# A graph attention layer on one core: x_r of 32 nodes as f32 rows beside the edge attributes, in one product over 64 rows

## The chip, the cores and the metric

The kernel runs on one core of a Trainium2 chip. The metric is device microseconds of one execution, on that core; the time before is the median of three runs. A core has five engines that run side by side and wait for each other by semaphores: PE (TensorE, matrix products out of SBUF into the PSUM banks; PEld in the profile is its loading of weights), DVE (VectorE), ACT (ScalarE), POOL (GpSimd, here nearly only the issuer of gathers from DRAM) and SP (which here issues all other transfers).

## The reference, cut to what matters

One pre-norm GATv2 layer with a feed-forward block over 12500 nodes of 128 features, 8 heads of 16 channels, and 400000 edges sorted by destination, with 32 attributes each:

```
h   = relu(layernorm(x));  g = LN1(h)
x_l = g @ W_l ;  x_r = g @ W_r ;  e = edge_attr @ W_e          # 128 wide
m     = leaky_relu(x_l[src] + x_r[dst] + e, 0.2)
alpha = sum over channels of m * att                            # 8 per edge
a     = softmax of alpha over the edges (and one self loop) of each dst
h2    = h + sum over edges of a * x_l[src] + bias
out   = x + h2 + gelu(LN2(h2) @ W1 + b1) @ W2 + b2
```

Self loops take the mean edge attribute. Everything is f32.

## The kernel before, in words

**Stages.** A first part (lines 701 to 761) normalises the nodes, computes x_l and writes it to DRAM (`xl_dram`, rows of 136 floats); meanwhile POOL gathers raw rows of x for 29 later groups of edges (L277, 116 gathers), from which x_l of those edges is recomputed later, so that the main loop need not gather them. x_r of later nodes is computed inside the main loop, four node tiles at a time (`xr_steps`, eight steps, one per round): it is split into three bf16 parts whose sum is the f32 value (`first`, `second`, `third`, L586 to L597), and stored to `xs_dram`, three rows of 128 bf16 per node.

**Main loop** (`window_edges`). The edges are cut into tiles of 128, two tiles make a unit (at most 16 destination nodes), two units a pair of 512 edges (at most 32 destination nodes, the window). There are 782 pairs. A round r runs every stage once, each for its own pair: the table `stages` (L1312) and `late_stages` say how many rounds a stage lies behind, and the order in the table is the order in which each engine gets its instructions; nothing is reordered. The node finish (`steps`, `soon`, `last_steps`) and the x_r and raw steps are put behind the stages in fixed rounds.

For pair c:
- `gather` (four rounds ahead, L907): four indirect transfers, 128 rows of `xl_dram` each, into the tile `xs`. Twelve `xs` tiles go round. The 29 pairs with recomputed rows load them from `late_dram` by SP instead, so 3009 gathers remain.
- `windows` (three rounds ahead, L923), on SP: once in four pairs the edge attributes `ea` (32 attributes of pair q on partitions 32q to 32q+31, 128 partitions in all) and `dlw`: on 96 partitions the distance of each edge's destination from the pair's first one, on 16 more from its unit's first one. Every pair: `xrw`, the 96 bf16 rows of its 32 nodes.
- `place` (one round ahead, L940): one DVE compare makes `ne`, 112 rows of 512 bf16 ones and zeros. Rows 3n to 3n+2 say that the edge goes to node n of the window; the 16 rows behind say that it goes to node n of its unit.
- `combine` (L954): in one PSUM bank `z`, four transposes of the gathered x_l, plus `xrw` times `ne` in bf16 (which picks x_r), plus `we_z` times `ea` in f32 (`we_z[q]` is W_e on the 32 rows of pair q and zero on the other 96).
- `slope` and `bend`: leaky relu, ACT and DVE, one round later, into `m`.
- `score` (two rounds behind, L976): in the bank `ab`, `farw` times `ne` (a huge number for the nodes of the unit that the edge does not go to) minus `m` times att. `lowest` (DVE) and `weigh` (ACT): minimum and exponentials `p` per node and head. `turn`, `keep_turned`, `collect`: transposes of `p`, and the weighted sums of `xs` into the bank `acc`. `own_heads` and `put` pick the own heads and store the sums.

Four rings of two PSUM banks each serve all this: `z`, `ab`, `pt_ps`, `acc`. The order of PE in a round is combine, turn, collect, score. DVE's is own_heads, lowest, bend, place, and then the steps of the node finish, among them `f_biases` (L1110, L1112) and `f_rest` (L1211), each an addition of two SBUF operands, and `f_out`, which takes a bank of the ring `ab` for two rounds. `f_z` reads x_r of its nodes from `xs_dram` and adds the three parts by 12 bf16 products with the identity for four tiles.

## Time and profile before

| what | value |
|---|---|
| three runs | 4013.26, 4021.4 (median), 4024.89 us |
| the profiled execution | 4009.67 us, of which the span 4007.9 |
| mean granted TensorE clock | 0.956 |
| busy: PE, DVE, ACT, POOL | 3550.4, 2540.8, 2185.3, 2993.8 us |
| moved by transfers | 566.02 MB, 141 GB/s on average |
| first and last gather of the main loop start at | 161.6 and 3950.8 us |

The profile is one execution. A row of a group gives line, engine, operation, output and inputs by the program's names, how often, then the busy time in us and the mean of one in ns, and behind the bar the idle time of that engine just before, with what ended it; `issue` there means that the engine waited for nothing that the profile shows. A row by line gives the shortest, median and longest of one in ns, and when the first and the last started. A row of the timeline gives start and length in us. The chain is followed back from the last instruction, at each step to what released it.

### The profile page before, as it was taken

To read this page: it belongs to the slowest core of one execution; us is meant where nothing else is said; L and a number is where in the kernel's file an instruction comes from. 1 tells how busy PE (TensorE), PEld (TensorE's weight loads), DVE (VectorE), ACT (ScalarE), POOL (GpSimd) and SP (SyncE) were. 2 spreads that over 40 slices of the span, in tenths; PEclk is the share of its full clock that TensorE was granted. 3 is DMA by queue.
4 is the path that set the end of the run, shared out by engine and by line. 5 is a ranking of instruction groups with operands and counts; after the bars stand their busy time and mean duration, and the time that the engine had idled before them with its cause. 6 is when DMAs were issued, how large, how long until landed. Compare 5 with 4: busy or idle time off the path is not lost.

```text
span 4007.9 us, 63213 instructions
## 1 busy us (share of the span) xinstructions
PE 3550.4 (89%) x19116; PEld 2520.3 (63%) x19315; DVE 2540.8 (63%) x5940; ACT 2185.3 (55%) x4768; POOL 2993.8 (75%) x3153
## 2 busy tenths in 40 slices
PE   3488998998889999998998999999989989998997
PEld 3356666666666666666666666666666666666665
DVE  7467676767666665665666666566666656566565
ACT  7445555555555545555555555556555455554554
POOL 7777777777777777777777777777777777777773
PEclk7699999999999999999999999999999999999998
DMA  7677787677656655555556556555556555655553
GB/s 215 207 186 193 197 206 201 173 178 170 166 122 132 128 125 127 126 124 125 118 126 133 125 124 128 128 125 120 127 118 130 125 115 123 127 118 124 125 116 72
DMA packets 650171, 566.02 MB, mean 141 GB/s; under 512 B 385806, under 2 KB 524925, under 8 KB 649581
## 3 DMA queue, kind: packets, MB, share of 16 engines
q1 hardware_dynamic: 549245, 344.42, 34.1%
q0 software_dynamic: 100000, 217.32, 27.4%
q8 instruction: 156, 2.56, 0.3%
q14 instruction: 194, 1.59, 0.1%
q10 hardware_dynamic: 576, 0.13, 0.0%
HBM read 492.44 MB, written 69.02 MB: 140 GB/s over the span
## 4 chain that ended last, share of the span: by engine, by line
PE 43%; DMA 21%; POOL 20%; issue 11%; DVE 1%; ACT 0%; SPq 0%; POOLq 0%; DVEq 0%; ACTq 0%
DMA xs<-xl_dram,src_sb 21%; POOL xs L915 20%; PE z L963 10%; PE acc L1021 9%; PE ab L981 8%; PE pt_ps L1007 5%; PE z L959 5%; PE z L962 2%; PE ab L980 1%; PE acc L1295 1%; PE acc L1270 1%; PE acc L1131 0%; PE pt_ps L581 0%; PE pt_ps L668 0%; PE acc L1126 0%
## 5 line engine op out<-in xcount | busy, mean ns | idle before, releaser
L915 POOL DMA_INDIRECT xs<-xl_dram,src_sb x3009 | 2873.2, 955 | 917.2 <-issue 792.8
L999 ACT ACTIVATE p<-ab,rec 128x256 f32<-128x256 f32 x1563 | 655.2, 471 | 1057.4 <-DVE rec L988 1041.1
L1030 DVE TENSOR_TENSOR own<-acc,diag 128x272 f32<-128x272 f32 x782 | 344.1, 440 | 1077.3 <-PE acc L1021 1061.6
L1021 PE MATMUL acc<-xs,pt 128*128 128x136 f32 x6250 | 881.0, 286 | 2.4 <-DVE f_o L1190 2.2
L959 PE MATMUL z<-ident,xs 128*128 128x128 f32 x3125 | 561.9, 283 | 342.6 <-DMA xs<-xl_dram,src_sb 338.6
L959 PEld LDWEIGHTS z<-ident,xs 128*128 128x128 f32 x3125 | 398.4, 142 | 741.1 <-DMA xs<-xl_dram,src_sb 410.8
L963 PE MATMUL z<-ea,we_z 128*128 128x512 f32 x1564 | 839.7, 620 | 0.1
L981 PE MATMUL ab<-m,negrep 128*128 128x512 f32 x1564 | 802.3, 595 | 11.4 <-issue 1.3
L1021 PEld LDWEIGHTS acc<-xs,pt 128*128 128x128 f32 x6250 | 809.3, 197 | 3.8 <-issue 3.5
L1012 ACT COPY pt<-pt_ps 128x512 f32<-128x512 f32 x782 | 455.1, 582 | 591.0 <-PE pt_ps L1007 581.6
L1007 PEld LDWEIGHTS pt_ps<-ident,p 128*128 128x128 f32 x3125 | 410.9, 147 | 439.3 <-issue 394.4
L988 DVE TENSOR_REDUCE rec<-ab 128x2 f32<-128x512 f32 x781 | 540.4, 692 | 124.0 <-PE ab L981 116.6
L974 DVE TENSOR_TENSOR m<-z,zs 128x512 f32<-128x512 f32 x782 | 532.8, 681 | 87.2 <-ACT zs L969 85.7
L969 ACT ACTIVATE zs<-z 128x512 f32<-128x512 f32 x782 | 472.6, 604 | 44.1 <-DMA xs<-xl_dram,src_sb 35.7
L1007 PE MATMUL pt_ps<-ident,p 128*128 128x128 f32 x3125 | 492.7, 283 | 1.2 <-ACT p L999 1.2
L1036 DVE TENSOR_REDUCE rec<-own 128x34 f32<-128x272 f32 x782 | 340.9, 436 | 26.7
L963 PEld LDWEIGHTS z<-ea,we_z 128*128 128x128 f32 x1564 | 308.1, 197 | 32.7
L981 PEld LDWEIGHTS ab<-m,negrep 128*128 128x128 f32 x1564 | 301.6, 193 | 40.2 <-issue 4.3
L962 PE MATMUL z<-ne,xrw 128*128 128x512 bf16 (+1 forms) x781 | 304.8, 390 | 0.2 <-DMA xs<-xl_dram,src_sb 0.2
L945 DVE TENSOR_SCALAR ne<-dlw,nid 112x512 bf16<-112x512 bf16 x782 | 288.2, 369 | 13.5 <-DMA dlw<-du_dram 13.5
L980 PE MATMUL ab<-ne,farw 128*128 128x512 bf16 x585 | 223.8, 383 | 2.5 <-ACT p L999 1.6
L277 POOL DMA_INDIRECT raw<-in_x,src_raw x116 | 116.6, 1005 | 38.0 <-issue 34.1
(246 smaller groups left out, 2317.4 us busy)
## 6 DMA issues: line engine op xcount, KB each, us to landing
dlw<-dc_dram SPq DMA_DIRECT2D x196, 384.0 KB
ea<-in_ea_t SPq DMA_DIRECT2D x196, 256.0 KB
ea_s<-in_ea_t SPq DMA_DIRECT2D x98, 512.0 KB
xs<-xl_dram,src_sb POOLq DMA_INDIRECT x3009
state<-rec SPq DMA_DIRECT2D x1563, 9.0 KB
xrw<-xs_dram SPq DMA_DIRECT2D x782, 24.0 KB
state<-empty SPq DMA_DIRECT2D x28, 504.0 KB
f_st<-state SPq DMA_DIRECT2D x48, 288.0 KB
```

Of the source, the lines that this page charges most:

```text
L915: nc.gpsimd.indirect_dma_start(out=xs[:, j, :], out_offset=None, in_=xl_dram, in_offset=bass.IndirectOffsetOnAxis(ap=src_sb[:, c * KP + j ...
L959: nc.tensor.matmul(z[:, j * P : (j + 1) * P], d["xs"][:, j, 0:P], ident, start=(j == 0), stop=False, is_transpose=True)
L962: nc.tensor.matmul(z[:, :e], xrw[c % NV], d["ne"][:, :e], start=False, stop=False)
L963: nc.tensor.matmul(z[:, :e], we_z[:, c % QP, :], d["ea"][:, :e], start=False, stop=True)
L969: nc.scalar.activation(d["zs"][:, :e], d["z"][:, :e], AF.Copy, scale=SLOPE)
L974: nc.vector.tensor_tensor(d["m"][:, :e], d["z"][:, :e], d["zs"][:, :e], op=OP.max)
L981: nc.tensor.matmul(ab[:, :e], negrep.rearrange("p n h -> p (n h)"), d["m"][:, :e], start=False, stop=True)
L988: nc.vector.tensor_reduce(d["rec"][:, :, CX], d["ab"].rearrange("p (u e) -> p u e", e=U), AX.X, OP.min)
L999: nc.scalar.activation(d["p"][:, us], d["ab"][:, us], AF.Exp, bias=d["rec"][:, i, CX:SH], scale=-1.0)
L1007: nc.tensor.transpose(d["pt_ps"][:, js], d["p"][:, js], ident)
L1012: nc.scalar.copy(d["pt"][:, :e], d["pt_ps"][:, :e])
L1021: nc.tensor.matmul(d["acc"][:, i, :], d["pt"][:, j * P : (j + 1) * P], d["xs"][:, j, :], start=(j == js[0]), stop=(j == js[-1]),)
```

## The change

- x_r is no longer split. `xr_steps` has six steps: `keep` copies the product to SBUF in f32 and `store` writes it to `xr_dram`, one row of 128 floats per node. The window of a pair is 32 rows of 512 bytes.
- A pair now uses one half of the 128 partitions, even pairs rows 0 to 63, odd pairs rows 64 to 127. In its half, 32 rows hold the edge attributes and 32 rows the ones and zeros for the nodes, now f32 and written by `place` into the tile `ea` itself. The matching weights `zw` hold W_e on 32 rows and the 32 x_r rows behind; `combine` makes one f32 product over these 64 rows in place of the bf16 product and the f32 product over 128 rows.
- The 16 rows for the nodes of the unit lie in the other half (for even pairs rows 64 to 79, for odd ones rows 0 to 15). `place` makes them for two pairs at once, in `ne`, by a bf16 compare over 96 partitions, once in two pairs. The product of `farw` with them is a stage of its own, `apart`, right behind `combine` and over the other 64 rows; it opens the bank `ab`, and `score` adds the f32 product.
- `windows` issues, once in four pairs, two transfers for `ea` and four for `dl` (32 rows of window distances and 16 of unit distances per half) in place of one and two; each pair's window goes to its half of `zw`.
- `f_z` adds x_r by four f32 products with the identity in place of 12 in bf16.
- The memsets of `xrw` on POOL go; DVE prepares `zw`, `ne` and `dl`. The constants for the third parts, `ident_b` and `we_z` go, others for the halves come.

```diff
-NS = 3
+HALF = P // 2
-XR_STEPS = 8
+XR_STEPS = 6
...
-        def first(d):
+        def keep(d):
             n = d["n"]
-            xr = d["b"][:, 0 : n * P].rearrange("p (t f) -> p t f", f=P)
-            d["parts"] = pool.tile([P, GN, NS, P], BF16, name="xr_parts")[:, 0:n]
-            nc.scalar.copy(d["parts"][:, :, 0, :], xr)
-            nc.vector.tensor_sub(tile_of(d, "left", 0), xr, d["parts"][:, :, 0, :])
-
-        def second(d):
-            nc.scalar.copy(d["parts"][:, :, 1, :], d["left"][:, 0 : d["n"]])
-
-        def third(d):
-            nc.vector.tensor_sub(d["parts"][:, :, 2, :], d["left"][:, 0 : d["n"]], d["parts"][:, :, 1, :])
+            d["xr"] = pool.tile([P, GN, XW], F32, name="xr_rows")[:, 0:n, 0:P]
+            nc.scalar.copy(d["xr"], d["b"][:, 0 : n * P].rearrange("p (t f) -> p t f", f=P))
...
-        for t in xrw:
-            nc.gpsimd.memset(t, 0.0)
+        for t in zws:
+            nc.vector.tensor_copy(t, weh)
         for t in nes:
-            nc.vector.memset(t, 1.0)
+            nc.vector.memset(t, 0.0)
+        for t in dls:
+            nc.vector.memset(t, float(NW))
...
+                ea = load.tile([P, QP // 2, EPR], F32, name="ea")
+                dl = dls[c // QP % ND]
+                for i in range(2):
+                    h, at = i * HALF, (c + i) * EPR
+                    nc.sync.dma_start(
+                        ea[h : h + DE], bass.AP(
+                            tensor=ea_t.tensor, offset=ea_t.offset + at, ap=[[e_pad, DE], [2 * EPR, QP // 2], [1, EPR]]
+                        ),
+                    )
+                    for rs, of in ((slice(h + DE, h + DE + CW), dc_dram), (slice(HALF - h, HALF - h + NW), du_dram)):
+                        nc.sync.dma_start(
+                            dl[rs], bass.AP(
+                                tensor=of.tensor, offset=of.offset + at,
+                                ap=[[0, rs.stop - rs.start], [2 * EPR, QP // 2], [1, EPR]],
+                            ),
+                        )
...
         def place(c):
 
             d = pairs[c]
-            n, q = sum(edges_of(c)), c % QP * EPR
-            ne = nes[c % NN]
-            nc.vector.tensor_scalar(
-                ne[0 : NC3 + NW, :n],
-                d["dlw"][:, q : q + n],
-                nid[0 : NC3 + NW],
-                None,
-                op0=OP.is_equal,
-            )
-            d["ne"] = ne
+            rs = slice(d["half"].start + DE, d["half"].stop)
+            nc.vector.tensor_scalar(d["ea"][rs], d["dl"][rs], nid[rs], None, op0=OP.is_equal)
+            if c % 2 == 0:
+                nc.vector.tensor_scalar(d["ne"][0 : P - DE], d["dl"][0 : P - DE], nid[0 : P - DE], None, op0=OP.is_equal)
...
-            nc.tensor.matmul(z[:, :e], xrw[c % NV], d["ne"][:, :e], start=False, stop=False)
-            nc.tensor.matmul(z[:, :e], we_z[:, c % QP, :], d["ea"][:, :e], start=False, stop=True)
+            rs = d["half"]
+            nc.tensor.matmul(z[:, :e], d["zw"][rs], d["ea"][rs, :e], start=False, stop=True)
             d["z"] = z
+
+        def apart(c):
+            d, e = pairs[c], sum(edges_of(c))
+            d["ab"] = ps2.tile([P, EPR], F32, name="ab")
+            rs = d["other"]
+            nc.tensor.matmul(
+                d["ab"][:, :e], farw.rearrange("p n h -> p (n h)")[rs], d["ne"][rs, :e], start=True, stop=False
+            )
...
-            ab = ps2.tile([P, EPR], F32, name="ab")
-            nc.tensor.matmul(ab[:, :e], farw.rearrange("p n h -> p (n h)"), d["ne"][:, :e], start=True, stop=False)
-            nc.tensor.matmul(ab[:, :e], negrep.rearrange("p n h -> p (n h)"), d["m"][:, :e], start=False, stop=True)
-            d["ab"] = ab
+            nc.tensor.matmul(d["ab"][:, :e], negrep.rearrange("p n h -> p (n h)"), d["m"][:, :e], start=False, stop=True)
...
             (0, combine),
+            (2, apart),
             (4, turn),
```

126 lines of the change are left out of this document (55 added, 71 removed).

## The prediction

> **What bounds the kernel now.** I read the table of engines first, then the chain that ended last, then the rows of POOL and PE, then the timeline. The table says PE 89%, POOL 75%; the chain is shared out between PE, DMA and POOL, so it names no bound.
>
> ```profile
> PE 3550.4 (89%) x19116; PEld 2520.3 (63%) x19315; DVE 2540.8 (63%) x5940; ACT 2185.3 (55%) x4768; POOL 2993.8 (75%) x3153
> PE 43%; DMA 21%; POOL 20%; issue 11%; DVE 1%; ACT 0%; SPq 0%; POOLq 0%; DVEq 0%; ACTq 0%
> L915 POOL DMA_INDIRECT xs<-xl_dram,src_sb x3009 | 2873.2, 955 | 917.2 <-issue 792.8
> L959 PE MATMUL z<-ident,xs 128*128 128x128 f32 x3125 | 561.9, 283 | 342.6 <-DMA xs<-xl_dram,src_sb 338.6
> L962 PE MATMUL z<-ne,xrw 128*128 128x512 bf16 (+1 forms) x781 | 304.8, 390 | 0.2 <-DMA xs<-xl_dram,src_sb 0.2
> L945 DVE TENSOR_SCALAR ne<-dlw,nid 112x512 bf16<-112x512 bf16 x782 | 288.2, 369 | 13.5 <-DMA dlw<-du_dram 13.5
> ```
>
> The L915 row decides. A gather takes 955 ns and 917.2/3009 = 305 ns lie idle before it, put down to nothing but issuing: 1.26 us each. POOL's timeline shows this beat from the first gather at 161.6 us to the last at 3950.8 without one wait longer than 0.3 us: 3009 x 1.26 = 3790 us of a span of 4007.9. POOL is full, though its busy share says 75%. PE has 339 us in which it waits for gathered rows (L959): it is the follower. So what counts is what makes a gather late. The rows for that (by line the shortest, median and longest; then pieces of the timeline: start, length, engine):
>
> ```profile
> L915 POOL DMA_INDIRECT xs<-xl_dram,src_sb x3009: 940/944/2289, 161.6 to 3950.8; - x189
> L945 DVE TENSOR_SCALAR ne<-dlw,nid x782: 248/345/592, 170.9 to 3956.0; 112x512 bf16<-112x512 bf16 x196
> ...
> 40.27 2.15 DVE L398 CAST df<-dc 112x3841 f32<-112x3841 int32 x1
> 40.52 2.72 POOL L277 DMA_INDIRECT raw<-in_x,src_raw  x1 [0.30 <-issue]
> ...
> 2657.57 0.95 POOL L915 DMA_INDIRECT xs<-xl_dram,src_sb  x1 [0.30 <-issue]
> 2658.74 0.34 DVE L945 TENSOR_SCALAR ne<-dlw,nid 112x512 bf16<-112x512 bf16 x1
> 2658.83 1.07 POOL L915 DMA_INDIRECT xs<-xl_dram,src_sb  x1 [0.30 <-issue]
> ...
> 3632.44 0.34 DVE L945 TENSOR_SCALAR ne<-dlw,nid 112x512 bf16<-112x512 bf16 x1
> 3632.52 2.29 POOL L915 DMA_INDIRECT xs<-xl_dram,src_sb  x1 [0.30 <-issue]
> 3632.70 0.69 DVE L1110 TENSOR_TENSOR h_sb<-h_sb,bias_r 128x512 f32<-128x512 f32 x1
> 3633.30 0.69 DVE L1112 TENSOR_TENSOR f_x<-f_x,b_r 128x512 f32<-128x512 f32 x1
> ```
>
> Some DVE work holds a gather back. The cast ends at 42.42; the gather that starts at 40.52 ends 1.78 us late, which is 42.42 - 40.52 - 0.13. At 2658.83 the DVE compare ends 0.25 us into the gather, and the gather is 0.12 late. At 3632.52 three DVE instructions without a gap end at 3633.99, and the gather is 1.35 late (3633.99 - 3632.52 - 0.13 = 1.34). The rule: a gather needs something that DVE work on SBUF alone (a compare, copy or cast; or two SBUF inputs) also takes. If such work began more than 0.08 us before the gather and is unfinished 0.13 us into it, the gather is late by the rest. Work with an input in PSUM (L974, L988, L1030) delays nothing. All gathers' lateness together is 3009 x (955 - 944) = 33 us; the rule applied to every such DVE instruction of the loop gives 33 us too.
>
> With starts spread evenly over the beat of 1.25 us, work of length D costs (D - 0.21)^2 / (2 x 1.25) per instruction. For L945 (0.345) that is 7.3 ns; where nothing else of the kind is near, the trace shows 8.
>
> **The change, part by part.** The sum is made against the profiled execution: 4009.67 us, span 4007.9; the median of the three runs, 4021.4, lies 11.7 above it.
>
> (1) The six memsets of xrw leave POOL ahead of its first gather: -0.9 us (0.93 in the timeline), all on the path. The other start-up edits (counting patterns, constants, memsets and copies on DVE) lie beside the raw gathers or POOL's lead of several rounds: 0, bounded by 1 either way.
>
> (2) PE loses the bf16 product with the x_r window (390 ns x 782 = 305 us), and the mask's product (383 ns) now stands behind the f32 product on the other 64 rows: 0 to 300 us more. The f32 product keeps 512 columns in two passes, 2 x 620 ns. On the path: 0, since PE already waits 339 us for gathers and will wait longer. Were that cover gone, 305 us would come back.
>
> (3) apart takes its bank ab earlier, ahead of turn and collect. It waits for the same exponentials that turn waits for (1.2 us in the whole run), so 0. Once a node group (24 times) f_out holds the other bank and collect stands behind for some 3 us; POOL is ahead by several rounds of buffers, so hidden. In the drain after the last gather (57 us) it may cost 2 us, and two pairs with 0.4 us less product give 1 to 2 back: 0, bounds -2 to +2.
>
> (4) SP issues 10 transfers for four pairs where it issued 7: two for ea, four for dl, still four of the window. At 0.4 to 0.6 us an issue (L926, L932, L936) that adds up to 2 us in 20; SP is issuing for about a third of the time and these loads lead by three rounds. The bytes of dl fall from 448 to 192 KB, of the window from 24 to 16. 0; without that lead combine would wait, which PE's idle time again covers. f_z goes from 12 bf16 products to 4 in f32 (eight passes of 0.28 against 0.83 us together), 24 times: hidden.
>
> (5) place. The old compare goes: 782 x 7.3 ns = -5.7 us. The subtraction L597 (685 ns, both inputs in SBUF, 24 times in the loop) goes: 17 alone at (0.685 - 0.21)^2 / 2.5 = 90 ns, and 7 behind L1211, where it makes a late gather some 0.43 later (up to 0.6): -4.5.
>
> New is, for every pair, a compare of 32x512 bf16 that writes f32. No row shows it. Low end: it runs like the f32 copy of 512 columns out of PSUM (L651, 681 ns), which delays no gather: 0. Otherwise its length follows the f32 compares of 128 columns (L380, 281 ns) and the slope between the long cast and one of 128 columns (L355, 207 ns), (2154 - 207)/(3841 - 128) = 0.524 ns: 281 + 384 x 0.524 = 482 ns. Cost (0.482 - 0.21)^2 / 2.5 = 29 ns, x 782 = +22.7. I take this: the cast mixes two types too and holds POOL.
>
> Each even pair also keeps a bf16 compare, 345 ns: 391 x 7.3 = +2.9 if POOL can slip in between the two. If they count as one hold of 0.482 + 0.345 - 0.085 = 0.74 us, an even pair costs (0.53)^2 / 2.5 = 112 ns: 391 x (112 + 29) = 55 in place of 26. Followers with two inputs (L1112 behind L1110) let nothing through; of compares and casts, the four L380 in a row did and the run L354 to L132 did not. I take the slip: L380 is the nearest form.
>
> Sum: -0.9 - 5.7 - 4.5 + 22.7 + 2.9 = +14.5. On 4009.7 that is 4024; on the median 4036.
>
> DVE grows by some 0.3 us in a round of 5.0 in which it works 3.1 (314.68 us of the 500 from 2000 us on): still hidden as occupancy.
>
> The Trainium skill, SBUF — State Buffer, section Who interferes with whom, says that Vector work in a two-port mode and GpSimd exclude each other for a whole instruction. By that alone every old compare costs a gather its full 345 ns, 270 us, and the change would add 782 x 0.482 + 391 x 0.345 - 270 = 242 us, 4263. The trace has 33 us for everything, so this gets no chance of its own. VectorE: DVE Perf Modes of the Trainium skill, section Two Vector instructions with no wait between them, says that an instruction whose output starts in another group of 32 partitions waits for the earlier one to finish; by it the two compares would not overlap, which favours the sum with the slip, 4036, over 4065. No run here shows such a pair.
>
> **Rivals.** (a) The two compares chain: 4021 + 44 = 4065. For it: L354 to L132. (b) The f32 compare holds nothing of POOL's: 4021 - 0.9 - 5.7 - 4.5 + 2.9 = 4013, not slower. It decides at this one instruction. For it: it touches 32 partitions and widens 16 to 32 bits, which no row does. Against: the cast. (c) PE is the bound after all, and its 305 us come off: 3716. Against: POOL's beat never breaks. (d) POOL's other use of the port matters: compares that start 0.47 to 0.69 us into a gather last up to 592 ns, so POOL holds them there. A compare of 345 already running then never made the gather late; one of 482 or 740 might, by up to its surplus of 0.14 to 0.4 us in a third of the pairs: +40 to +100 more, 4075 to 4135.
>
> **How the numbers follow.** Forecast 0.41, (a) 0.23, (b) 0.24, (c) 0.03, (d) 0.09. The likeliest gives 4036, by itself 4028 to 4046. The range takes in (b) down to 4008 and (a) up to 4075 and leaves out (c) and most of (d). No change means within 0.3%, 12 us (4009 to 4033), about what a measurement here can tell. Slower: two thirds of the forecast, (a) and (d), 0.59. Same: the rest of the forecast and two thirds of (b), 0.31. Faster: (c) and the rest of (b), 0.10.
>
> **What would show it.** After: the new compare near 0.48 us; the mean of L915's successor above 955 by 3 to 8 ns, its median still 944; PE's busy time down by 300 us or more and its wait for gathered rows up by as much; the last gather 10 to 20 us later; the tail behind it within 2 us of 57. A compare near 0.7 us and a mean near 952 would mean (b); a mean of 968 or more, (a) or (d). Waits of POOL for PE or DVE above 0.3 us would overturn the whole reading.

## The result, and the profile after

The changed kernel takes 4012.6 us (median of 13 runs, 4002.6 to 4016.0), the kernel before 4021.3 (13 runs, 4013.3 to 4024.9): ratio 0.9978, 95% interval 0.9970 to 0.9987. The forecast was 4036, slower. It is faster by 0.2%, inside the forecast's range of 4008 to 4075 but on the other side of no change; by the prediction's own measure, 0.3%, it is no change. The profiled execution takes 4002.62 us with a span of 4000.9, against 4009.67 and 4007.9: 7.0 us less span.

The page of the changed kernel answers the lines shown of before: the engines, then POOL's gathers, PE's wait for gathered rows, the product over 64 rows, the mask's product behind it, and the f32 compare of `place`.

```profile
PE 3562.0 (89%) x18434; PEld 2247.7 (56%) x18435; DVE 2814.9 (70%) x6281; ACT 2176.4 (54%) x4743; POOL 2990.0 (75%) x3146
L900 POOL DMA_INDIRECT xs<-xl_dram,src_sb x3009 | 2872.0, 954 | 917.3 <-issue 768.9
L954 PE MATMUL z<-ea,zw 64*128 64x512 f32 x1564 | 897.4, 654 | 2.4 <-DMA zw<-xr_dram 2.4
L950 PE MATMUL z<-ident,xs 128*128 128x128 f32 x3125 | 597.5, 286 | 325.2 <-DMA xs<-xl_dram,src_sb 293.8
L941 DVE TENSOR_SCALAR ea<-dl,nid 32x512 f32<-32x512 bf16 x782 | 394.8, 505 | 28.7 <-DMA dl<-dc_dram 3.4
L961 PE MATMUL ab<-ne,farw 64*128 64x512 bf16 x782 | 305.8, 391 | 17.7 <-ACT p L995 17.3
```

POOL still sets the beat: 3009 gathers with 917.3/3009 = 305 ns idle before each, and PE still waits for them (293.8 us). The instructions by line (shortest, median and longest in ns; first and last start in us) show how late the gathers are:

```profile
L900 POOL DMA_INDIRECT xs<-xl_dram,src_sb x3009: 940/944/1975, 158.0 to 3945.5; - x189
L941 DVE TENSOR_SCALAR ea<-dl,nid x782: 475/485/734, 168.0 to 3948.5; 32x512 f32<-32x512 bf16 x196
L943 DVE TENSOR_SCALAR ne<-dl,nid x391: 348/350/573, 169.8 to 3943.9; 96x512 bf16<-96x512 bf16 x196
```

The new compare has a median of 485 ns (forecast 482), and an undisturbed gather still takes 944. In what follows, the lateness of a kernel is the busy time of its gathers beyond 3009 x 0.944 = 2840.5 us. It is 2873.2 - 2840.5 = 32.7 us before and 2872.0 - 2840.5 = 31.5 after. The span's 7.0 us are then: 3.6 ahead of the first gather of the loop (161.6 to 158.0 us), 1.7 between first and last gather, 1.7 in the tail behind the last (57.1 to 55.4).

So the loop hardly moved. Yet it is not the same lateness. Counted gather by gather (those over 8 ns late, by the DVE instructions that stand at them; the counts add up to about 1 us more than the busy times), it falls into two groups (of the first, 1.2 us before and 0.6 after stand at other DVE work):

| us of lateness | no addition in it, nearly all compares | an addition (L1110, L1112, L1211 before; L1106, L1108, L1205 after) or the subtraction L597 in it |
|---|---|---|
| before | 4.9 | 28.8 |
| after | 24.4 | 8.3 |

The first column comes out near the 25.6 us forecast, but partly by luck. By the prediction's rule, at the moment 0.13 us into a gather, the f32 compare costs 19.2 us in sum (22.7 forecast) and the bf16 one 0.03 (2.9 forecast). Another 4.5 us come from 62 gathers that are held at a second moment: the f32 compare begins 0.35 to 0.46 us into the gather and is unfinished at 0.82, and the gather is late by the rest, to within 8 ns, at most 0.12 us. One of them (start, length, engine; DVE and POOL only, as in all pieces of the timeline below that name no other engine):

```profile
502.10 1.04 POOL L900 DMA_INDIRECT xs<-xl_dram,src_sb  x1 [0.30 <-issue]
502.55 0.48 DVE L941 TENSOR_SCALAR ea<-dl,nid 32x512 f32<-32x512 bf16 x1
```

A compare of 345 ns that begins there has ended by 0.82. This is the mechanism of the prediction's rival (d), at 4.5 us instead of 40 to 100.

What the forecast did not have is the other column: 20.5 us less, where it had 4.5 for the subtraction. Three stretches of the timeline show the difference. The kernel before, a compare with the two bias additions behind it:

```profile
1118.40 0.39 DVE L945 TENSOR_SCALAR ne<-dlw,nid 112x512 bf16<-112x512 bf16 x1
1118.71 0.67 DVE L1110 TENSOR_TENSOR h_sb<-h_sb,bias_r 128x512 f32<-128x512 f32 x1
1118.97 1.83 POOL L915 DMA_INDIRECT xs<-xl_dram,src_sb  x1 [0.30 <-issue]
1119.30 0.68 DVE L1112 TENSOR_TENSOR f_x<-f_x,b_r 128x512 f32<-128x512 f32 x1
```

The changed kernel, in an odd pair (the f32 compare alone):

```profile
3472.49 0.48 DVE L941 TENSOR_SCALAR ea<-dl,nid 32x512 f32<-32x512 bf16 x1
3473.01 0.69 DVE L1106 TENSOR_TENSOR h_sb<-h_sb,bias_r 128x512 f32<-128x512 f32 x1
3473.41 1.11 POOL L900 DMA_INDIRECT xs<-xl_dram,src_sb  x1 [0.30 <-PE pt_ps L1003]
3473.62 0.68 DVE L1108 TENSOR_TENSOR f_x<-f_x,b_r 128x512 f32<-128x512 f32 x1
```

And in an even pair, where the bf16 compare stands behind the f32 one:

```profile
2690.45 0.35 DVE L943 TENSOR_SCALAR ne<-dl,nid 96x512 bf16<-96x512 bf16 x1
2690.72 0.68 DVE L1106 TENSOR_TENSOR h_sb<-h_sb,bias_r 128x512 f32<-128x512 f32 x1
2690.85 1.98 POOL L900 DMA_INDIRECT xs<-xl_dram,src_sb  x1 [0.31 <-issue]
2691.32 0.68 DVE L1108 TENSOR_TENSOR f_x<-f_x,b_r 128x512 f32<-128x512 f32 x1
```

Before, the first addition starts while the compare is still running (118.71 against 118.79), and the gather is 0.89 us late: until the *second* addition ends (1119.98 - 1118.97 - 0.13 = 0.88). In the odd pair L941 writes partitions 96 to 127 and L1106 starts 32 ns after it has ended; the gather is 0.17 late, until the *first* addition ends (3473.70 - 3473.41 - 0.13 = 0.16), though the second has begun by then. In the even pair the old picture is back: no gap, 1.03 us late.

The theory that was tested, T: POOL's beat and what DVE adds to it decide; a compare opens a hold that all DVE work behind it prolongs as long as no gap lies between, and the 32-ns gap behind the new compare cuts that. Rivals: R1, the gain is PE's, from the saved product; R2, it is the removed subtraction alone; R3, the start-up.

### The profile page after: what moved, and what is told of

Its sections match the earlier page's. It is cut to its first block, busy times and chain, and to the rows that moved or that the text cites. A ratio compares the mean times of both kernels' runs of the same rounds, so it can differ in the third digit from the quotient of the medians.

```text
span 4000.9 us, 63115 instructions
## 1 busy us (share of the span) xinstructions
PE 3562.0 (89%) x18434; PEld 2247.7 (56%) x18435; DVE 2814.9 (70%) x6281; ACT 2176.4 (54%) x4743; POOL 2990.0 (75%) x3146
## 4 chain that ended last, share of the span: by engine, by line
PE 39%; DMA 21%; POOL 21%; issue 14%; DVE 4%; SPq 1%; ACT 1%; POOLq 0%; DVEq 0%; ACTq 0%
POOL xs L900 19%; DMA xs<-xl_dram,src_sb 18%; PE z L954 10%; PE acc L1017 9%; PE ab L978 7%; PE pt_ps L1003 6%; PE z L950 4%; POOL raw L278 1%; DMA state<-rec 1%; PE acc L1289 1%; DMA zw<-xr_dram 1%; PE acc L1264 1%; SPq L920 0%; DMA raw<-in_x,src_raw 0%; DVE rec L984 0%
## 5 line engine op out<-in xcount | busy, mean ns | idle before, releaser
L900 POOL DMA_INDIRECT xs<-xl_dram,src_sb x3009 | 2872.0, 954 | 917.3 <-issue 768.9
L954 PE MATMUL z<-ea,zw 64*128 64x512 f32 x1564 | 897.4, 654 | 2.4 <-DMA zw<-xr_dram 2.4
L950 PE MATMUL z<-ident,xs 128*128 128x128 f32 x3125 | 597.5, 286 | 325.2 <-DMA xs<-xl_dram,src_sb 293.8
L950 PEld LDWEIGHTS z<-ident,xs 128*128 128x128 f32 x3125 | 407.3, 143 | 771.3 <-DMA xs<-xl_dram,src_sb 439.9
L978 PE MATMUL ab<-m,negrep 128*128 128x512 f32 x1564 | 828.1, 612 | 0.0
L1003 PEld LDWEIGHTS pt_ps<-ident,p 128*128 128x128 f32 x3125 | 339.6, 144 | 611.0 <-issue 516.2
L984 DVE TENSOR_REDUCE rec<-ab 128x2 f32<-128x512 f32 x781 | 539.6, 691 | 28.8 <-PE ab L978 28.2
L1003 PE MATMUL pt_ps<-ident,p 128*128 128x128 f32 x3125 | 533.5, 295 | 0.6 <-ACT pt L1008 0.6
L941 DVE TENSOR_SCALAR ea<-dl,nid 32x512 f32<-32x512 bf16 x782 | 394.8, 505 | 28.7 <-DMA dl<-dc_dram 3.4
L1032 DVE TENSOR_REDUCE rec<-own 128x34 f32<-128x272 f32 x782 | 340.9, 436 | 26.7
L961 PE MATMUL ab<-ne,farw 64*128 64x512 bf16 x782 | 305.8, 391 | 17.7 <-ACT p L995 17.3
L954 PEld LDWEIGHTS z<-ea,zw 64*128 64x128 f32 x1564 | 234.2, 187 | 117.2 <-issue 56.5
L978 PEld LDWEIGHTS ab<-m,negrep 128*128 128x128 f32 x1564 | 252.6, 200 | 3.0 <-issue 3.0
L943 DVE TENSOR_SCALAR ne<-dl,nid 96x512 bf16<-96x512 bf16 x391 | 147.4, 377 | 13.8 <-DMA dl<-du_dram 1.3
```

Source lines behind the costliest of these rows:

```text
L900: nc.gpsimd.indirect_dma_start(out=xs[:, j, :], out_offset=None, in_=xl_dram, in_offset=bass.IndirectOffsetOnAxis(ap=src_sb[:, c * KP + j ...
L941: nc.vector.tensor_scalar(d["ea"][rs], d["dl"][rs], nid[rs], None, op0=OP.is_equal)
L950: nc.tensor.matmul(z[:, j * P : (j + 1) * P], d["xs"][:, j, 0:P], ident, start=(j == 0), stop=False, is_transpose=True)
L954: nc.tensor.matmul(z[:, :e], d["zw"][rs], d["ea"][rs, :e], start=False, stop=True)
L978: nc.tensor.matmul(d["ab"][:, :e], negrep.rearrange("p n h -> p (n h)"), d["m"][:, :e], start=False, stop=True)
L984: nc.vector.tensor_reduce(d["rec"][:, :, CX], d["ab"].rearrange("p (u e) -> p u e", e=U), AX.X, OP.min)
```

## The experiments

Ratios are to the kernel before on the same chip. Part of the runs were on three other chips, where the kernel before itself takes 4741 to 4794 us and POOL's beat does not decide; they stand at the end.

**A gap in the kernel before.** One tiny memset to partitions 32 to 63 behind each compare:

```
             d["ne"] = ne
+            nc.vector.memset(gap[32:64, :], 0.0)
```

> The kernel before, with one DVE memset of 32 partitions x 1 element behind each compare of place; nothing is left out. On a chip where POOL's beat decides (PE waits for gathered rows): theory T (in the gap ahead of an instruction whose output starts in another group of partitions POOL gets in, so the chain of compare and additions is cut): the additions' share of the lateness (22 us with the compare in it) falls to 6 to 12 us, the time by 10 to 17 us, ratio 0.996 to 0.9975. R1 (the gain comes from the product that PE is spared), R2 (from the removed subtraction), R3 (from the start-up): ratio 1.000 and lateness 33 us.

Measured: 3991.3 us against 4012.8, ratio 0.9949 (0.9935 to 0.9962). The groups of the gathers and of the memset (busy time, mean, idle time ahead):

```profile
L916 POOL DMA_INDIRECT xs<-xl_dram,src_sb x3009 | 2856.0, 949 | 917.1 <-issue 787.2
L954 DVE MEMSET gap<- 32x1 f32 x782 | 46.1, 59 | 38.6
```

The timeline behind one compare:

```profile
1448.86 0.34 DVE L946 TENSOR_SCALAR ne<-dlw,nid 112x512 bf16<-112x512 bf16 x1
1449.26 0.06 DVE L954 MEMSET gap<- 32x1 f32 x1
1449.33 0.69 DVE L1112 TENSOR_TENSOR h_sb<-h_sb,bias_r 128x512 f32<-128x512 f32 x1
1449.71 1.13 POOL L916 DMA_INDIRECT xs<-xl_dram,src_sb  x1 [0.30 <-issue]
1449.94 0.68 DVE L1114 TENSOR_TENSOR f_x<-f_x,b_r 128x512 f32<-128x512 f32 x1
```

The lateness falls from 32.7 to 15.5 us and the longest gather from 2.29 to 1.46; the additions and the subtraction fall from 28.8 to 10.2. The time falls by 21.5 us, more than the 10 to 17 expected. The gather at 1449.71 is late by 0.19, to the first addition's end (1450.02 - 1449.71 - 0.13 = 0.18). DVE does 782 instructions more and the kernel is 0.5% faster. R1, R2 and R3 said 1.000: PE's products, the subtraction and the start-up are as before. So this gain has none of them as its reason: the gap alone does it. What the subtraction, the start-up and PE's product have in the change itself is measured below.

**The subtraction alone.**

```
-            nc.vector.tensor_sub(d["parts"][:, :, 2, :], d["left"][:, 0 : d["n"]], d["parts"][:, :, 1, :])
+            nc.scalar.copy(d["parts"][:, :, 2, :], d["left"][:, 0 : d["n"]])
```

> The kernel before, with the subtraction of the third part replaced by a copy on ACT (the third bf16 part of x_r is then not the remainder: that part of the computation is left out). On a chip where POOL's beat decides: the predicted step, -4.5 us, ratio 0.9989, with the additions' lateness as before; the two traces' own reading, -4 to -6 us; R2 (all that the change gained beside the price of the new compare): -30 us, ratio 0.9925; R1, R3: 1.000.

Measured: ratio 0.9984 (0.9975 to 0.9993), 6.3 us on the medians; the gathers' busy time is 2866.9, lateness 26.4, that is 6.3 less. The additions keep 22.0 us. The step was sized 4.5 and is 6.3; R2's 30 us are not there.

**The f32 compare in a form that holds nothing.** The compare also adds up its output into one column, which is not used:

```
-            nc.vector.tensor_scalar(d["ea"][rs], d["dl"][rs], nid[rs], None, op0=OP.is_equal)
+            nc.vector.tensor_scalar(
+                d["ea"][rs], d["dl"][rs], nid[rs], 0.0, op0=OP.is_equal, op1=OP.add, accum_out=hits[rs]
+            )
```

> The changed kernel with the compare that writes f32 in the form that also adds up its output into one column (the sum is not used). Theory T: if this form works at one element per cycle, it takes about 0.68 us plus an instruction that reads the sum (near 0.06 to 0.2 us), as the f32 copy of 512 columns out of PSUM does (0.68 us), and it no longer holds what the gathers need: their lateness falls from 31.6 us by the compare's 19 to 23 us, so on a chip where POOL's beat decides the time falls by 18 to 23 us against the changed kernel (3980 to 3985 us profiled). DVE's busy time grows by 0.25 us x 782 = 200 us, to about 3000 us (75%), off the path. Rival Rb (the compare holds nothing as it is): no gain, and the longer compare costs nothing either: 4002 us. Rival Rc (a longer compare holds POOL for its whole length all the same): (0.68 - 0.21)^2 / 2.5 = 88 ns x 782 = 69 us instead of 23, so 46 us more: 4048 us.

Measured: one run, 3989.7 us against 4011.4 for one run of the kernel before, ratio 0.9946. Groups of instructions, of which the second is the read of the sum:

```profile
L942 DVE TENSOR_SCALAR_CACHE_REDUCE ea<-dl,nid 32x512 f32<-32x512 bf16 x782 | 578.5, 740 | 38.8 <-DMA dl<-dc_dram 13.6
L942 DVE DVE_READ_ACCUMULATOR ea<-dl,nid 32x1 f32 x782 | 57.8, 74 | 0.0
```

The compare is half as long again, 740 ns instead of 505, and its share of the lateness goes from 19.2 us at the first moment and 4.5 at the second to 0.03: the rivals of no price (Rb) and of a price by length (Rc) fall. The Trainium skill, SBUF — State Buffer, section Who interferes with whom, excepts the accumulating form from the instructions that can take the ports shared with GpSimd; this run agrees, with 0.03 us for 782 of them. But the whole lateness falls only by 13.4 us, to 18.1 (the gathers take 2858.6 us), where 18 to 23 less were expected, and the span by 13.0 (3987.9 against 4000.9, on another chip), because the additions go back up from 8.3 to 16.1. T had not said so. With only a bf16 compare ahead of them the chains of the even rounds are as before; in odd rounds the additions are late by their own length, and where 24 pairs of them fall in the beat differs from kernel to kernel.

**The additions apart.** On top of that form, `place` moves ahead of `bend`, whose input lies in PSUM, and the two bias additions stand in different rounds:

```
+            (-1, place),
             (1, bend),
             (3, weigh),
-            (-1, place),
...
             (-2, f_biases),
+            (-3, f_biases_x),
```

> The changed kernel with the accumulating form of the f32 compare, with place moved ahead of bend (whose input lies in PSUM) so that no addition stands behind a compare, and with the two bias additions of a node group one round apart instead of back to back. T: by (D - 0.21)^2 / 2.5, 48 bias additions of 0.685 us apart cost 0.09 us each, 4.3 us, instead of the 11.3 us that they cost with their neighbours in the kernel with the accumulating form alone; the 24 residual additions 2.2 instead of 4.8; the bf16 compare 391 x 7.3 ns = 2.9. So the lateness is 9 to 13 us after 20.8, and the time 8 to 12 us below that kernel: ratio to the kernel before 0.9915 to 0.9930. R1 (PE decides): no gain over the changed kernel, 0.998. Without the chain's part of T (each addition costs what it costs wherever it stands): ratio 0.9945, as the accumulating form alone.

Measured: 3987.0 us, ratio 0.9935 (0.9921 to 0.9948); gathers 2854.6 us, lateness 14.1. The gain over the accumulating form alone is about half of that expected: the longest gather is down from 2.2 to 1.8 us, but gathers with an addition in them cost 12.4 us where the formula gave 6.5. The edit did not cut the chain in even pairs: the bf16 compare now stands ahead of `bend`, and the addition behind `bend`, without a gap:

```profile
2501.27 0.35 DVE L946 TENSOR_SCALAR ne<-dl,nid 96x512 bf16<-96x512 bf16 x1
2501.54 0.68 DVE L976 TENSOR_TENSOR m<-z,zs 128x512 f32<-128x512 f32 x1
2502.08 1.56 POOL L901 DMA_INDIRECT xs<-xl_dram,src_sb  x1 [0.30 <-issue]
2502.14 0.68 DVE L1210 TENSOR_TENSOR f_x<-f_x,h_sb 128x512 f32<-128x512 f32 x1
```

The gather comes while `bend` runs and is held to the end of the addition behind it (2502.82 - 2502.08 - 0.13 = 0.61). `bend` itself, with an input in PSUM, holds nothing: of 88 gathers that came while it ran behind such a compare and with a gap behind it, one was late, by 0.02 us. But the hold passes through it. Of 18 gathers that came so with an addition next, nine were held to the addition's end, together 7.1 of the 12.4 us; why not the other nine is open. Without these nine, 5.3 us are left.

**And each addition in halves, with gaps.**

```
+        def by_halves(to, other, n):
+            for t in range(0, n, 2):
+                ts = slice(t, min(t + 2, n))
+                nc.vector.memset(gap[32:64, :], 0.0)
+                nc.vector.tensor_add(to[:, ts], to[:, ts], other(ts))
+            nc.vector.memset(gap[32:64, :], 0.0)
```

> The changed kernel with the accumulating form of the f32 compare, place ahead of bend, the bias additions a round apart, and each of the three additions of a node group in two halves of 256 elements with a DVE memset of 32 partitions x 1 element ahead of, between and behind them. On a chip where POOL's beat decides: T: a half takes about 0.42 us and costs (0.42 - 0.21)^2 / 2.5 = 18 ns, 144 of them 2.5 us, where the whole additions cost 12.4 us in the kernel without halves; the lateness above 944 ns falls from 16.9 to 8 to 12 us and the time by 5 to 10 us: ratio to the kernel before 0.9910 to 0.9925. Without the gaps' part of T (two halves back to back hold as long as one whole): no gain, 0.9935. R1 (PE decides): 0.998.

Measured: 3978.7 us against 4013.9, ratio 0.9914 (0.9901 to 0.9928).

The group of the gathers:

```profile
L902 POOL DMA_INDIRECT xs<-xl_dram,src_sb x3009 | 2845.9, 946 | 917.3 <-issue 775.5
```

The lateness is down to 5.4 us (8 to 12 expected), no gather takes more than 1.19 us, and the kernel beats both others: 0.9% off before, with DVE busier (3037 us against 2541). What is left is the beat itself, 3008 x 1.249 = 3757 us of a loop of 3762.

**The f32 compare in two halves**, one ahead of `bend`, one behind:

```
+            (-1, place_first),
             (1, bend),
```

> The changed kernel with the f32 compare in two of 256 columns, the first ahead of bend and the second behind it. On a chip where POOL's beat decides: T: each half takes 348 ns (281 + 128 x 0.524) and costs (0.348 - 0.21)^2 / 2.5 = 7.6 ns, so 2 x 782 of them cost 12 us where the whole compares cost 19 to 23: 7 to 11 us less lateness than the changed kernel's 34 us above 944 ns, ratio to the kernel before 0.9950 to 0.9965. If a compare's cost goes with its length rather than with the square of what is over 0.21 us: 2 x 348 against 505 ns, 7 us more, ratio 0.9995. Rb (the compare holds nothing): 0.998.

Measured: ratio 0.9984 (0.9975 to 0.9993), no gain over the changed kernel. The group of the half compares:

```profile
L940 DVE TENSOR_SCALAR ea<-dl,nid 32x256 f32<-32x256 bf16 x1564 | 589.1, 377 | 53.3 <-DMA dl<-dc_dram 3.4
```

The part that the formula speaks of came out: the f32 compares' share fell from 19.2 to 9.7 us (12 expected), and all compares' from 24.4 to 18.7, although DVE spends 194 us more on them. The additions rose from 8.3 to 17.6. They were not touched and stand behind the same gaps; where they fall in the beat moved. So the square law fits a compare to within a fifth, and a gain of 6 us is less than what 24 pairs of additions may give or take.

**The two compares of the even pairs exchanged**, the bf16 one first:

```
+            if c % 2 == 0:
+                nc.vector.tensor_scalar(d["ne"][0 : P - DE], d["dl"][0 : P - DE], nid[0 : P - DE], None, op0=OP.is_equal)
             nc.vector.tensor_scalar(d["ea"][rs], d["dl"][rs], nid[rs], None, op0=OP.is_equal)
-            if c % 2 == 0:
-                nc.vector.tensor_scalar(d["ne"][0 : P - DE], d["dl"][0 : P - DE], nid[0 : P - DE], None, op0=OP.is_equal)
```

> The changed kernel with the two compares of the even pairs in the other order, the 96-row one first. On a chip where POOL's beat decides: T: behind the f32 compare, whose output starts at partition 32, there is a gap in even rounds too, so the additions' lateness in even rounds (most of the 8 us left) falls by 2 to 5 us; ratio to the kernel before 0.9965 to 0.9975. R1, R2, R3: as the changed kernel, 0.998.

Measured: ratio 1.0002 (0.9993 to 1.0011): a miss, worse than the changed kernel by some 10 us. The additions did what T says, 8.3 to 4.3 us. But the compares rose from 24.4 to 41.7. The timeline shows why:

```profile
728.52 0.94 POOL L900 DMA_INDIRECT xs<-xl_dram,src_sb  x1 [0.30 <-DMA xs<-xl_dram,src_sb]
...
729.05 0.53 DVE L942 TENSOR_SCALAR ne<-dl,nid 96x512 bf16<-96x512 bf16 x1
729.59 0.48 DVE L943 TENSOR_SCALAR ea<-dl,nid 32x512 f32<-32x512 bf16 x1
729.77 1.14 POOL L900 DMA_INDIRECT xs<-xl_dram,src_sb  x1 [0.30 <-issue]
```

A compare that starts 0.46 to 0.7 us into a gather is itself stretched: here 0.53 us instead of 0.34. In 67 such even rounds (starts between 0.5 and 0.7) the bf16 compare ends at 1.06 us into the gather, whenever it began; so the f32 compare starts at 1.07, which is 0.18 us ahead of the next gather, and makes it 0.18 us late nearly every time. POOL's second use of what both want lines the compares up, and in this order it lines the longer one up with the worst place. In the changed kernel the stretched one is the f32 compare; it ends at 1.19, the short one starts at 1.22, less than 0.08 us ahead of the gather, and costs nothing there.

**PE given its product back**, with zero weights:

```
+            nc.tensor.matmul(z[:, :e], none, nes[0][:, :e], start=False, stop=False)
             nc.tensor.matmul(z[:, :e], d["zw"][rs], d["ea"][rs, :e], start=False, stop=True)
```

> The changed kernel with a bf16 product of zero weights over 512 columns added to every pair's z, as large as the one that the change took away: 0.39 us x 782 = 305 us more of PE. On a chip where POOL's beat decides: T: PE's waits for gathered rows fall from 294 us to some 50 or below, the time stays within 0 to 8 us of the changed kernel's, ratio to the kernel before 0.997 to 1.000; the loop's gathers keep 1.26 us. R1 (the product that PE is spared gives the gain): all of it back, 1.000, or 300 us more where PE has no cover left: 1.07.

Measured: 4008.0 us against 4013.0, ratio 0.9987 (0.9978 to 0.9996); the changed kernel's interval is 0.9970 to 0.9987. Groups of the new product and of PE's wait for gathered rows:

```profile
L956 PE MATMUL z<-ne,none 128*128 128x512 bf16 x782 | 299.3, 383 | 3.0 <-DMA zw<-xr_dram 2.2 <-DVE ne L945 0.8
L952 PE MATMUL z<-ident,xs 128*128 128x128 f32 x3125 | 558.6, 282 | 230.2 <-DMA xs<-xl_dram,src_sb 203.9 <-DMA zw<-xr_dram 5.5 <-DMA ea<-in_ea_t 5.3
```

299 us of product come in, and the loop from first to last gather is 3789.1 us against 3787.5. PE's wait for gathered rows goes from 293.8 to 203.9 us, not to 50, and its busy time from 3562 to 3654: 90 us each, since the other products are shorter in the records (L950's, here L952, 558.6 us for 597.5). On the path it is nothing that this measurement can tell; the cover holds.

**The six POOL memsets put back** ahead of the loop's first gather:

```
+        for i in range(6):
+            nc.gpsimd.memset(once.tile([P, P], BF16, name=f"idle{i}"), 0.0)
```

> The changed kernel with six POOL memsets of 128x128 bf16 put back ahead of the loop's first gather. Predicted step: 0.9 us later, the memsets' own time. What the two traces show: the first gather 2.9 us later (161 instead of 158.0 us, 3.2 us after the last raw gather instead of 0.3), because POOL also stood idle for 2 us around them. If the start-up's gain has nothing to do with them: 0 to 0.9 us.

POOL's timeline at that place, in the kernel before:

```profile
157.45 0.94 POOL L277 DMA_INDIRECT raw<-in_x,src_raw  x1 [0.30 <-issue]
160.50 0.93 POOL L892 MEMSET xrw<- 128x128 bf16 x6 [2.11 <-issue]
161.59 0.95 POOL L915 DMA_INDIRECT xs<-xl_dram,src_sb  x1 [0.15 <-issue]
```

In the changed kernel:

```profile
156.75 0.94 POOL L278 DMA_INDIRECT raw<-in_x,src_raw  x1 [0.30 <-issue]
158.00 0.94 POOL L900 DMA_INDIRECT xs<-xl_dram,src_sb  x1 [0.30 <-issue]
```

And with the memsets back:

```profile
158.27 0.94 POOL L278 DMA_INDIRECT raw<-in_x,src_raw  x1 [0.31 <-issue]
161.32 1.06 POOL L873 MEMSET idle<- 128x128 bf16 x6 [2.10 <-issue]
162.54 0.95 POOL L902 DMA_INDIRECT xs<-xl_dram,src_sb  x1 [0.16 <-issue]
```

From the end of the last raw gather to the first of the loop it is 3.2 us before, 0.3 after, 3.3 with the memsets back: 3.0 us, of which the memsets themselves take 1. The other 2.1 are POOL's idle time ahead of the first memset.

**On the other chips.** There the same kernels gave: the gap 1.0011 (1.0001 to 1.0021), the subtraction gone 1.0001 (0.9989 to 1.0013), the exchanged compares 1.0021 (1.0010 to 1.0033), the halves 1.0039 (1.0025 to 1.0053), the best version 1.0056 (1.0039 to 1.0072), PE's product back 1.0029 (1.0019 to 1.0039); the memsets 4738.7 us in one run against 4744.2. The changed kernel itself was not run there. The timeline of PE and of POOL in the last of these:

```profile
2031.05 0.74 PE L1019 MATMUL acc<-xs,pt 128*128 128x136 f32 x5 [1.05 <-issue]
...
2031.48 0.95 POOL L902 DMA_INDIRECT xs<-xl_dram,src_sb  x1 [2.12 <-remote]
```

PE stands still for 1.05 us in the midst of eight products of one line, the last five of which are shown, and POOL's next gather starts only then. In each of the runs with the gap and without the subtraction some 430 gathers start over 0.25 us later than the beat has them, some 695 us together. What stops PE there the trace does not say, and it stays open. There the time of a gather counts for little. The profiled executions of kernels made from the changed one also show a lower granted clock there, 0.895 to 0.909, than the two made from the kernel before, 0.930 and 0.940; so why the best version is slower there, by its DVE work or otherwise, is open too. Two kernels were run there only. In one the f32 compare was left out:

```
-            nc.vector.tensor_scalar(d["ea"][rs], d["dl"][rs], nid[rs], None, op0=OP.is_equal)
```

> The changed kernel without the compare that writes f32: the one-hot rows of the edge attributes stay zero, so x_r is left out of the scores. Price of that compare as predicted: 23 us; T: 18 to 23 us less than the changed kernel, 3980 to 3985 us profiled, ratio to the kernel before near 0.993; the lateness falls from 31.6 to about 10 us, and the additions behind place in odd rounds may chain again with each other (up to 4 us back). Rival Rb (the compare holds nothing): the same time as the changed kernel, ratio 0.998. R1 (PE decides): 0.998 too, since PE's work is unchanged.

Measured: 1.0009 (0.9998 to 1.0019), so the time tells nothing; but its gathers' lateness by the count is 17.9 us, of which 16.3 with additions in it. In even pairs the chain behind the bf16 compare is as before. In odd pairs no compare is left, and the additions follow `bend` without a gap:

```profile
1752.56 0.69 DVE L974 TENSOR_TENSOR m<-z,zs 128x512 f32<-128x512 f32 x1
1753.17 0.68 DVE L1107 TENSOR_TENSOR h_sb<-h_sb,bias_r 128x512 f32<-128x512 f32 x1
1753.38 1.28 POOL L903 DMA_INDIRECT xs<-xl_dram,src_sb  x1 [0.30 <-issue]
1753.77 0.69 DVE L1109 TENSOR_TENSOR f_x<-f_x,b_r 128x512 f32<-128x512 f32 x1
```

The gather is 0.34 us late, to the end of the first addition (1753.85 - 1753.38 - 0.13 = 0.34), and so are all six that came to their moment there: without a compare ahead, additions without a gap do not hold as one. In the other kernel the gap was put behind the even pairs' bf16 compare:

```
                 nc.vector.tensor_scalar(d["ne"][0 : P - DE], d["dl"][0 : P - DE], nid[0 : P - DE], None, op0=OP.is_equal)
+                nc.vector.memset(gap[32:64, :], 0.0)
```

> The changed kernel with a DVE memset of 32 partitions x 1 element behind the bf16 compare of the even pairs. T: in even rounds too the bias and residual additions no longer stand in a chain that a compare opened; a gather then waits for the end of one addition, not of all: the additions' lateness falls from 8.3 to 3 to 6 us, ratio to the kernel before 0.9965 to 0.9975. Rival: only the length of what DVE does in a row counts, not what opened it: as the changed kernel, 0.998. R1, R2, R3: 0.998.

Measured: 1.0011 (1.0000 to 1.0022), which tells nothing; the additions' lateness is about 4 us, as T has it, and no gather is held to a second addition's end.

What was expected of the other runs on those three chips:

> The kernel before, with one DVE memset of 32 partitions x 1 element behind each compare of place; nothing is left out. Theory T (POOL's beat decides; a DVE instruction whose output starts at another partition group starts only after the one ahead has ended, and in that gap POOL gets in between the compare and the bias additions or the residual addition that follow, so the chain is cut): the gathers' lateness falls from 33 us to 16 to 23 us and the time by 10 to 17 us, to a ratio near 0.997, with PE, SP and all transfers as they were. Rival R1 (the gain of the change comes from the bf16 product that PE is spared): no less than the kernel before, ratio 1.000, lateness 33 us. Rival R2 (it comes from the removed subtraction alone): ratio 1.000, lateness 33 us. Rival R3 (it comes from the start-up): ratio 1.000.

> The kernel before, with the subtraction of the third part replaced by a copy on ACT: the third bf16 part of x_r is then not the remainder, so this kernel leaves out that part of the computation. As predicted for that step: -4.5 us, ratio 0.9989, lateness 33 to 28.5 us. T: the lateness that the two traces put down to it, 4 to 6 us, ratio 0.9985 to 0.999, and the bias additions stay as late as before (17 us with their neighbours). R2 (the whole gain of the change is the subtraction, before the price of the new compare): -30 us, ratio 0.9925. R1, R3: 1.000.

> The changed kernel with the two compares of the even pairs in the other order: the 96-row one first, then the one that writes f32. T: in even rounds what follows the compares then starts behind an output at partition 32, with a gap, as in odd rounds, so the chains that are left there (bias additions 6.2 us, residual addition 2.0 us of lateness) are cut: 2 to 5 us less lateness than the changed kernel's 31.6, ratio to the kernel before 0.9965 to 0.9975. Rivals R1, R2, R3: as the changed kernel, 0.998.

> The changed kernel with the accumulating form of the f32 compare, place ahead of bend and the bias additions a round apart, and now each of the three additions of a node group in two halves of 256 elements with a DVE memset of 32 partitions x 1 element ahead of, between and behind them. T: a half takes about 0.42 us (0.685 less 256 elements at 1.04 ns) and costs (0.42 - 0.21)^2 / 2.5 = 18 ns, 144 of them 2.5 us, where the whole additions cost 12.4 us in the kernel without halves; with 2.5 for the bf16 compare and 1.6 for the rest the lateness falls from 16.9 to 6 to 9 us and the time by 8 to 11 us: ratio to the kernel before 0.9905 to 0.9920 where POOL's beat decides. Without the gaps' part of T (two halves back to back hold as long as one whole): no gain, 0.9935. R1 (PE decides): 0.998.

> The changed kernel with the f32 compare in two of 256 columns, the first ahead of bend and the second behind it. T: each half takes 348 ns (281 + 128 x 0.524) and costs (0.348 - 0.21)^2 / 2.5 = 7.6 ns, so 2 x 782 of them cost 12 us where the whole compares cost 19 to 23: 7 to 11 us less lateness than the changed kernel's 34 us above 944 ns, ratio to the kernel before 0.9950 to 0.9965. If a compare's cost goes with its length rather than with the square of what is over 0.21 us: 2 x 348 against 505 ns, 7 us more, ratio 0.9995. Rb (the compare holds nothing): 0.998.

> The changed kernel with six POOL memsets of 128x128 bf16 put back ahead of the loop's first gather. Predicted step: 0.9 us later, the memsets' own time. What the two traces show: the first gather 2.9 us later (161 instead of 158.0 us, 3.2 us after the last raw gather instead of 0.3), because POOL also stood idle for 2 us around them. If the start-up's gain has nothing to do with them (the shorter lists of patterns and constants, the raw gathers' own lateness): 0 to 0.9 us.

> The changed kernel with a bf16 product of zero weights over 512 columns added to every pair's z, as large as the one that the change took away: 0.39 us x 782 = 305 us more of PE. T (POOL's beat decides): PE's waits for gathered rows fall from 294 us to some 50 or below, PE's busy time rises to about 3860 us of 4001, and the time stays within 0 to 8 us of the changed kernel's, ratio to the kernel before 0.997 to 1.000; the loop's gathers keep 1.26 us. R1 (the product that PE is spared gives the gain): all of it back, 1.000, or 300 us more where PE has no cover left: 1.07.

## Why the prediction was wrong, step by step

The bound was read rightly. POOL's beat decides on the chips of the main runs, PE follows, and in all eleven kernels there the loop, from first to last gather, less the lateness is 3755 to 3757 us (before 3789.3 - 32.7, after 3787.5 - 31.5, the gap 3772.0 - 15.5, the exchanged compares 3802.1 - 45.8, the best 3762.0 - 5.4): 3008 beats of 1.249 us.

(1) The memsets: forecast -0.9, measured -3.0 by putting them back (-3.6 at the first gather, with what the raw gathers ahead of it were earlier). POOL's 2.1 us of idle time ahead of them belonged to them; the step counted only their busy time.

(2) PE: 0 on the path, right; giving the product back moved the loop by 1.6 us. But "PE's busy time down by 300 us" was wrong: it went from 3550 to 3562. The bf16 product's 305 us are gone; the f32 product over 64 rows takes 58 us more than that over 128, the mask's product has 197 records more in this trace (82 us), and the other four kinds of products take 127 us more in sum; the rest lies in small groups. Why those are longer is open. The other sign named for it, PE's wait for gathered rows up by as much, failed too: it went from 339 to 294 us.

(3) The tail: 0 with bounds of 2, measured -1.7. The mask's product waits 17.3 us for the exponentials in the whole run, not 1.2, inside PE's cover.

(4) SP and the transfers: 0, right; PE waits 11 us for the window (8.6 at L950 and 2.4 at L954), inside its cover.

(5) The compares: the new one 485 ns for 482, both new ones together 24.4 us of lateness for 25.6, and in the runs with the memsets and with PE's product back 26.7 each; but 4.5 of the 24.4 are rival (d)'s, so the size fits partly by luck. The two slip apart, as taken: 32 ns lie between the end of L941 and the start of L943. The Trainium skill, VectorE: DVE Perf Modes, section Two Vector instructions with no wait between them, says that an instruction whose output starts in another group of 32 partitions starts only when the earlier ones have finished; the trace agrees, with these 32 ns. Rivals (a) and (b) are out. That (b)'s time, 4013, is the measured one is luck: its mechanism, a compare that holds nothing, is refuted by the 19.2 us. The removed compare alone was 4.9 for 5.7, the subtraction 6.3 for 4.5.

What failed is the sum of (5), in which the additions behind the compare have no term, and one sentence there: "Followers with two inputs (L1112 behind L1110) let nothing through". It was read off a kernel in which L1110 always stands behind L945 without a gap. The gathers that came to their moment, 0.13 us in, while the first bias addition ran can be followed in before, after and seven of the experiments. Where nothing but work without a gap lay between a compare and that addition, all 49 were held to the end of the second addition, to within 12 ns. Behind a gap (31 to 32 ns after the f32 compare or its accumulator read, 14 ns after the memset), all 48 for which the addition had begun at least 0.05 us ahead of the gather were held only to the end of the first, to within 6 ns; the 24 for which it began later were not late. So it is not the two inputs that let nothing through; it is the compare ahead, whose hold goes on as long as work follows it without a gap. The forecast priced each removed and added instruction by itself and left out that the new compare, by where it writes, changes what the instructions behind it cost: -20.5 us in the additions and the subtraction, where it had -4.5. It used the rule on outputs in another group of partitions for the two compares, but not for the additions behind them.

How much of the 20.5 is the gap's is known less well. With the same order on DVE the additions cost 8.3, 8.4 and 6.9 us (after, the memsets, PE's product back); behind the same gaps, but with the f32 compare halved or accumulating, 17.6 and 16.1, against 22.0 in the kernel before without the subtraction. So part of it is where the 24 pairs of additions happen to fall in the beat.

With that the sum reads: start-up -3.6, compares +24.4 - 4.9 = +19.5, additions and subtraction -20.5, tail -1.7, together -6.3 against the 7.0 measured. The forecast's +14.5 is 21.5 off: 16.0 in the additions and the subtraction, 2.7 in the start-up, 1.7 in the tail, 0.4 in the compares, 0.7 unexplained. Rival (c) is refuted by the product put back. Rival (d)'s mechanism exists, at 4.5 us in the changed kernel. What (d) did not have, that a stretched compare moves the one behind it onto the next gather, adds 17 us when the compares are exchanged. The prediction's chances of the same time and of a faster one add up to 0.30 and 0.11, not 0.31 and 0.10.

## What to carry to other kernels

When one engine issues gathers at a fixed beat, price the DVE work by its runs without a gap, not by the instruction, and look at which instruction opens the run: a single 60-ns memset to other partitions behind each compare was worth 0.5% here, more than the whole change. Then look at when in the beat the work falls, since what stretches one instruction sets the start of the next. And see that the bound is the same on every chip that the kernel will run on: the best version here is 0.9% faster where the gathers' beat decides and 0.6% slower where PE stands still.

## What the runs showed of the hardware

- A DVE compare of bf16 or to f32 holds back a gather's start not only while it runs but through all DVE work that follows without a gap, two-input additions too: gathers up to 1.35 us late before, and 49 of 49 held to the end of a second addition. Work with an input in PSUM lets the hold through (nine gathers, 0.6 to 0.9 us late, with the additions apart). A gap of 14 or 32 ns ends it: 48 of 48 held to the first addition's end only.
- Two-input additions hold gathers by themselves as well, each to its own end: up to 0.52 us late behind the memset. The Trainium skill, SBUF — State Buffer, section Who interferes with whom, infers that such work takes only the read side and does not hold back the making of descriptors; these gathers are held all the same. They read their row numbers (`src_sb`) from SBUF; whether it is that reading or the descriptors that waits, no run here tells.
- A compare that starts 0.46 to 0.7 us into a gather is stretched by up to 0.25 us (485 to 734 ns for the f32 one) and ends at a fixed time in the gather (1.19 us for the f32 one, 1.06 for the bf16 one). One that starts a little earlier and ends later than 0.82 us into the gather makes the gather late by the rest (62 gathers, at most 0.12 us).
- The accumulating form of the same compare takes 740 ns and 74 for the read, and holds next to nothing (0.03 us in 782).
- Six POOL memsets between gathers cost 3.0 us, of which 2.1 are idle time ahead of the first.
